# Merged slot loads, a five-step layer 0 and a new end in a four-layer graph-network kernel

## The chip, the core and the metric

The kernel runs on one core of a Trainium2 chip. The metric is the device time of one execution in microseconds (us); a comparison uses the median of several runs. The engines are TensorE (PE; weight loads are listed apart as PEld), VectorE (DVE), ScalarE (ACT), GpSimd (POOL) and SyncE (SP), which here only issues DMAs. The core has 16 DMA engines. A DMA that SP or ACT issues goes onto that engine's own queue, and instructions stand in the order of each engine's program.

## The reference

`reference(x, adj, ...)` takes 128 graphs of 64 nodes with 128 channels (x is 128 x 64 x 128) and a weighted adjacency (128 x 64 x 64) in which about a quarter of the entries are not zero and below 6. Four layers follow one another, each as `x = layernorm(x + layer(x))`:

- layer 0: a filter network over distances. Each entry d of adj becomes 20 Gaussians, exp(coeff d^2); these go through a 20 x 128 matrix, softplus, and a 128 x 128 matrix, and are multiplied by a cosine cutoff. The resulting filter W (one 128-vector per edge) multiplies the neighbour's features y = x w_in2f and is summed over neighbours; two dense layers follow.
- layer 1: the same with 64 Gaussians of other centres, other weights, and the entry of adj squared in place of the cutoff.
- layer 2: a two-hop graph convolution with elu, D^-1/2 (A + I) D^-1/2.
- layer 3: one normalised graph convolution with relu.

Everything is float32.

## The kernel before

Two graphs make a pair, which fills the 128 partitions: graph b on partitions 64b to 64b + 63. There are 64 pairs, in 8 sets of 8. Graphs are sorted by their number of edges, and within a graph the edges are compacted into "slots", so that only entries that count are worked on. A slot row holds, for all edges of one graph, the distance (d), the neighbour's index (j) and the weight (w). The slots per graph are `GSLOTS`: in layer 0 1080, 1092, 1044, 1020, 1008, 1008, 996 and 948 for the eight sets, in layer 1 1260, 1260, 1212, 1212, 1200, 1176, 1152 and 1140. Compaction writes the rows to DRAM; `later_loads` (L1365) reads them back per pair, each row broadcast over the partitions of its graph. In layer 0 a row of d is read in three thirds, each onto 20 (the last 24) partitions of the graph's 64, since 20 Gaussians are computed on each; in layer 1 onto all 64.

Before the steps, about 69 us load inputs and weights and compact the first set. Then `sparse_stack` (L613) runs a list of steps, the pairs two by two ("double pairs", 32 in each layer). A step takes a chunk of slots of both graphs. `chunks_of` (L68) gives the chunks: two per pair where the size is at most 1024 (layer 0, sets 3 to 7: four steps per double pair), three where it is more (sets 0 to 2: six steps), and in layer 1 five per double pair, whose middle step takes its slots from both pairs. A step is:

- `filter_in` (L1827): PE multiplies the Gaussians with the first matrix into PSUM (px), ACT takes Exp; `softplus` (ACT Ln);
- `gather` (L1856) of the step before: PE multiplies the features with a one-hot matrix (pg), ACT copies it (m<-pg); the one-hot matrix of a pair is made by DVE (`one_hot`, L1803) from j and w;
- `filter_out` (L1842) of the step before that: PE, second matrix (pw); `message` (L1882): DVE multiplies filter and features; `slot_sums` (L1912, L1916): DVE sums over the edges of each node.

`gaussians` (L1790) runs on ACT one to three pairs ahead. Beside the steps run generators that are advanced a few yields at a time: `early` (the compaction of later sets), `side`, `befores`, `nodes` and `convs` (dense layers per group of four pairs, layer norms, and layers 2 and 3 in `graph_convs`), `sums`, `last` (the same for the small groups at the end) and `stores`. `TURNS` says for each kind of step how far each is advanced, which pair's loads are issued (`load` for d, `late` for j and w, two or three pairs ahead) and which pair's Gaussians are computed. `in_order` (L648) makes each engine's order that of emission. The buffers: d and w three pairs deep, j two. In layer 1 the groups are of four pairs, except that the last set is split: q = 14 has pairs 0 to 3 of it, q = 15 two, 16 and 17 one each.

In the layer norm of a four-pair group (`layernorm`, L1448) GpSimd computes the reciprocal root with pow (L1460, L1461) and scales the four pairs (L1466); in the small groups ACT does it with Ln and Exp, and DVE scales. After the last step the remaining generators are advanced in turn until they are empty; all of them share two PSUM banks (`bank`, L1424). GpSimd writes the finished rows to their places in the output with indirect DMAs (L995).

Of the kernel before, what the change touches and what calls it, by code (L numbers as in the profile page):

```python
# [19 lines left out]
P = 128  # L20
# [46 lines left out]

def chunks_of(layer, size):  # L68

    if layer == 1:  # L70
        wide = -(-2 * size // 5)
        return (wide, wide, size - 2 * wide, size - 2 * wide, wide, wide)
    n = 2 if size <= 1024 else 3
    return (size // n,) * (2 * n)
# [538 lines left out]
def sparse_stack(ctx: ExitStack, tc: tile.TileContext, t: dict, out: bass.AP, flag):  # L613
# [122 lines left out]
    def dram_ap(ap, offset, dims):  # L736
        return bass.AP(tensor=ap.tensor, offset=ap.offset + offset, ap=dims)
# [118 lines left out]

    at_step = [0]

    def at_phase(k):
        while phase[0] not in (k, None):  # L860
            yield

    def steps_later(n):
        to = at_step[0] + n
        while at_step[0] < to:
            yield
# [498 lines left out]
    def later_loads(n):  # L1365


        layer, p = pair_at(n)
        s = p // 8
        size = GSLOTS[layer][s]  # L1370
        at = (p % 8) * 2 * size
        assert (layer, s) in stored, "slots are read before they are written"
        d = edge.tile([P, MAX_SLOTS], F32, tag="d", name=f"d_{n}", bufs=3)
        j = edge.tile([P, MAX_SLOTS], BF16, tag="j", name=f"j_{n}")
        w = edge.tile([P, MAX_SLOTS], F32, tag="w", name=f"w_{n}", bufs=3)

        def load(to, name, first, n):
            engine.dma_start(to, dram_ap(slots[layer, name][s], first, [[0, to.shape[0]], [1, n]]))  # L1378

        third = size // 3  # L1380
        d = d[:, 0 : size if layer else third]
        for b in range(2):
            rows, first = slice(A * b, A * (b + 1)), at + b * size
            engine = nc.sync
            if layer == 1:
                load(d[rows], "d", first, size)
            else:
                for k, end in enumerate((NG0, 2 * NG0, A)):
                    engine = nc.scalar if n == 0 and b * k == 0 else nc.sync
                    load(d[A * b + NG0 * k : A * b + end], "d", first + k * third, third)  # L1390

        def late():
            nonlocal engine
            engine = nc.sync
            for b in range(2):
                rows, first = slice(A * b, A * (b + 1)), at + b * size
                load(j[rows, 0:size], "j", first, size)
                load(w[rows, 0:size], "w", first, size)

        return (d, j, w), late  # L1400

# [19 lines left out]

    def bank(name, n=GS):  # L1424
        ps = ps_n.tile([P, 512], F32, tag="n", name=name)[:, 0 : n * P]
        return ps, ps.rearrange("p (s c) -> p s c", s=n)

# [7 lines left out]
    def tiled(name, n, q):  # L1435


        tag = f"c{q % 2}" if n == GS else f"c_{q}"
        return rings[0].tile([P, n * P], F32, tag=tag, name=f"{name}_{q}", bufs=4)

# [7 lines left out]
    def layernorm(y, dst, n, name, quick=False):  # L1448

        stats = node.tile([P, GS, 6], F32, tag="st", name=f"st_{name}", bufs=4)[:, 0:n]  # L1450
        mv = node.tile([P, GS, 2], F32, tag="mv", name=f"mv_{name}", bufs=4)[:, 0:n]
        for s in range(n):
            nc.vector.bn_stats(stats[:, s, :], y[:, s, :])
            nc.vector.bn_aggr(mv[:, s, :], stats[:, s, :])  # L1454
            if s + 1 == GS // 2 < n and not quick:
                yield
        rstd = node.tile([P, GS], F32, tag="rs", name=f"rs_{name}", bufs=4)[:, 0:n]
        yield
        if n == GS:
            nc.gpsimd.tensor_scalar(rstd, mv[:, :, 1], LN_EPS, None, ALU.add)  # L1460
            nc.gpsimd.tensor_tensor(rstd, rstd, neg_half[:, 0:n], ALU.pow)  # L1461
        else:
            act(rstd, mv[:, :, 1], AF.Ln, bias=ln_eps)
            act(rstd, rstd, AF.Exp, scale=-0.5)
        for s in range(n):
            (nc.gpsimd if n == GS else nc.vector).tensor_scalar(  # L1466
                dst[:, s, :], y[:, s, :], mv[:, s, 0:1], rstd[:, s : s + 1],
                ALU.subtract, ALU.mult,
            )
        yield  # L1470
# [128 lines left out]
    def node_after(layer, q, agg):  # L1599
# [48 lines left out]
        if layer == 1:  # L1648
            if n < GS:
                yield from graph_convs(q)  # L1650
            else:
                convs[q % 2].append(graph_convs(q))

    def elu(ps, bias, i, q, also=()):

# [40 lines left out]

        act(to, ps, AF.Copy)

    normals = {}

    def normals_of(q):

# [9 lines left out]
    def graph_convs(q):  # L1712
# [14 lines left out]
            return y  # L1727

        if n == GS:
            yield from at_phase(6)  # L1730
            scaled(2, q)
        flat, ps = bank(f"gx_{q}", n)
        for s in range(n):
# [17 lines left out]
        yield True  # L1751
        nT3 = by_pair(tiled("nTs3", n, q)) if n == GS else normals[3, q]
        h1 = yield from elu(flat, g["b1"], 1, q, normal(3, q, nT3) if n == GS else ())
        y2 = yield from times("hw2", lambda s: h1[:, s, :], lambda s: g["W2"])
        _, ps = bank(f"o2_{q}", n)
        for s in range(n):
# [4 lines left out]
        yield  # L1761
        yield from layernorm(z, xs, n, f"2_{q}")
        if n == GS:
            yield from at_phase(2)
        y3 = yield from times("sup", lambda s: xs[:, s, :], lambda s: nT3[:, s, :])
        flat, ps = bank(f"o3_{q}", n)
        nc.tensor.matmul(
# [153 lines left out]
            else:  # L1921
                nodes.append(node_after(layer, q, agg))

    befores, nodes, convs, sums = deque(), deque(), (deque(), deque()), deque()
    small_groups, small = range(NP // GS - 1, len(GROUPS[1])), {}
    at_end = range(NP // GS - 2, len(GROUPS[1]))
    last = {q: deque() for q in small_groups}
# [69 lines left out]
    def steps_of(n):  # L1997


        layer, p = pair_at(n)  # L2000
        size = GSLOTS[layer][p // 8]
        cuts, at = [], 0
        for m in CHUNKS[layer][p // 8]:
            cuts.append([part_of(n + at // size, at % size, at % size + m)])
            at += m
        if layer == 1:
            cuts[2:4] = [cuts[2] + cuts[3]]
        for k, cut in enumerate(cuts):
            yield dict(
                id=f"{n}_{k}", layer=layer, w=layers[layer], n=n, k=k, beat=len(cuts), parts=cut,  # L2010
                phase=k + p // 2 % 2 * len(cuts),
                size=sum(x["cols"][1] - x["cols"][0] for x in cut),
                starts=[x["n"] for x in cut if x["cols"][0] == 0],
            )
# [13 lines left out]
            gauss=((1, 0), (1, 1), None, (2, 0), (2, 1), None),  # L2028
            end=(7,) * 6,
        ),  # L2030
        4: dict(
            sums=(2, 3, 2, 2), early=(6, 7, 6, 7), side=(2, 3) * 2,
            late=(2, None, 3, None), load=(2, None, 3, None),
# [7 lines left out]
            end=(10,) * 5,  # L2041
        ),
    }
    FREE, MORE = 8, 0
    BEFORES = {6: (3, 4, 7, 8, 9), 4: (2, 3, 5, 6, 7), 5: (7, 8, 9)}

    block = nc.cur_bb.bb.instructions
    past = [None] * 2
# [1 line left out]
    for i in range(len(steps) + 2):  # L2050
        c, c1, c2 = steps[i] if i < len(steps) else None, *past
        now = c or dict(steps[-1], k=i - len(steps), phase=i - len(steps), starts=[])
        n, k, beat, layer = now["n"], now["k"], now["beat"], now["layer"]
        turn = {name: values[k] for name, values in TURNS[beat].items()}
        phase[0], at_step[0] = now["phase"] if n < N - FREE else None, i

        if n >= N - 4:
            run(sums, (2, 2, 5, 4, 2)[k] if c is not None else 9)
        else:
            run(sums, turn["sums"])  # L2060
        run(early, 9 if i < 18 else turn["early" if n < NP - 8 else "end"])
# [18 lines left out]
        if c is not None:  # L2080
# [4 lines left out]
            for part_ in c["parts"]:  # L2085
                m, (_, q) = part_["n"], part_["at"]
                if part_["cols"][0] > 0:
                    continue
                if m + GS < N:
                    ahead(m)  # L2090
                if part_["s"] == min(1, len(range(NP)[GROUPS[layer][q]]) - 1):
                    load_nodes(layer, q)
                if m > 0:
                    one_hot(m)
                if layer == 1 and part_["s"] == 0 and q in last:
                    last[q].append(normals_of(q))
            filter_in(c)
            if len(c["parts"]) == 2 and n + 3 < N:
                slot_data[n + 3], late_loads[n + 3] = later_loads(n + 3)
# [1 line left out]
            gather(c1)  # L2101
        if c is not None and turn["late"] is not None and n + turn["late"] < N:
            late_loads.pop(n + turn["late"])()
        if layer == 1 and befores and (n >= N - 8 or phase[0] in BEFORES[beat]):
            slot(befores)
        if c is not None:
            softplus(c)
            if beat % 2 == 0 and k % (beat // 2) == beat // 2 - 1 and sines:

                sines.popleft()()  # L2110
        if layer == 0:
            slot(nodes)
            if befores and phase[0] in BEFORES[beat]:
                slot(befores)
        if c2 is not None:
            filter_out(c2)
        for queue in last.values():
# [2 lines left out]
            slot(nodes)  # L2120
        if c2 is not None:
            message(c2)
        for _ in range(1 + (n >= N - MORE)):
            if convs[0]:
                slot(convs[0])
        if c is not None and turn["gauss"] is not None:
            m, stage = n + turn["gauss"][0], turn["gauss"][1]
            for stage in range(begun.get(m, 0), stage + 1 if m < N else 0):
                gaussians(m, stage)
                begun[m] = stage + 1  # L2130
        for _ in range(1 + (n >= N - MORE)):
            slot(convs[1])
        for queue in last.values():
            slot(queue)
        past = [c, c1]
    phase[0] = None
    run(sums, -1)
    while nodes or convs[0] or convs[1] or any(last.values()) or stores:
        for queue in (*last.values(), nodes, *convs):
            slot(queue)  # L2140
        run(stores, 1)
    in_order(first, block[-1], (nc.tensor, nc.scalar, nc.vector, nc.gpsimd, nc.sync))

# [46 lines left out]
```

## Time and profile before

| | |
|---|---|
| median of 3 runs | 1578.65 us (1576.26 to 1581.45) |
| the profiled execution | 1577.26 us |
| its span, first to last instruction | 1575.4 us |
| first step begins | 69.3 us |
| set 3 begins; layer 1 begins | 346.8; about 728 us |
| last message ends; last norm ends | 1512.1; 1568.75 us |

The page lists the busy time of each engine as a share of the span, then the busy share in slices, the DMA queues, the chain of work that ended last, and the costliest groups of instructions. A group's line gives the code line, engine and operation, output<-inputs, shapes, the number, then busy us and mean ns, then the engine's idle time just before them and what ended it. The view of stretches gives, for each stretch of the span, its length, each engine's busy time with the number of instructions, the granted TensorE clock, the busy share of the 16 DMA engines and the GB/s they moved. The trace further holds each DMA packet with its size and time, and each increment of a DMA's semaphore.

The double pairs of sets 0 to 2 begin 22.0 us apart (from 170.9 us on), those of sets 3 to 7 19.06 us, those of layer 1 23 to 24 us.

### The profile page before, as it was taken

The numbers are of one execution on the slowest core, as the hardware profiler recorded it, in microseconds if no ns is written. First come the engines' busy times: TensorE is split into PE (matmuls) and PEld (weight loads), VectorE is DVE, ScalarE is ACT, GpSimd is POOL, SyncE is SP. The second block draws the span as 40 slices with busy tenths as digits, with TensorE's granted clock in tenths as the row PEclk, the third lists the DMA queues.
The fourth block names the chain that finished last, engine by engine and source line by source line (L and its number), as shares of the span: only waits on it lengthen the run. The fifth ranks groups of instructions, "written<-read, shape, count | busy, mean of one in ns | idle before, by whom it ended". The sixth has DMA issues, their size and how long they took to land.

```text
span 1575.4 us, 23201 instructions
## 1 busy us (share of the span) xinstructions
PE 1427.4 (91%) x6841; PEld 790.8 (50%) x6841; DVE 1316.5 (84%) x2895; ACT 1313.8 (83%) x1647; POOL 759.3 (48%) x1175
## 2 busy tenths in 40 slices
PE   1387999999989999999999999999999999998974
PEld 1143454554444445554444555555555655554553
DVE  8796988888989899788788888888888888878763
ACT  1366897989888989899999999999999999988742
POOL 2435256365564545333912334555544665555544
PEclk9999999999999999999999999999999999999985
DMA  6766454545555545447665655555555555654100
GB/s 205 258 139 137 101 136 116 129 123 136 130 142 124 141 130 135 125 114 167 155 152 142 143 132 132 147 133 136 139 130 138 139 132 131 150 132 106 31 7 23
DMA packets 122280, 205.60 MB, mean 131 GB/s; under 512 B 47956, under 2 KB 80034, under 8 KB 121506
## 3 DMA queue, kind: packets, MB, share of 16 engines
q1 hardware_dynamic: 113330, 188.40, 48.2%
q0 software_dynamic: 6576, 14.99, 2.9%
q8 instruction: 57, 0.93, 0.3%
q10 hardware_dynamic: 2240, 0.65, 0.2%
q14 instruction: 77, 0.63, 0.1%
HBM read 185.29 MB, written 18.64 MB: 129 GB/s over the span
## 4 chain that ended last, share of the span: by engine, by line
PE 61%; ACT 11%; DVE 9%; DMA 6%; issue 4%; SPq 2%; POOL 2%; another core or an unknown queue 1%; DVEq 0%; ACTq 0%; POOLq 0%
PE pw L1842 23%; PE px L1827 13%; PE pg L1856 11%; ACT h L955 5%; DVE m L1882 2%; DMA w<-w_dram 2%; DVE agg L1912 2%; DMA j<-j_dram 2%; ACT d L955 2%; PE y L1491 1%; PE hw L1722 1%; SPq L1378 1%; PE u L1615 1%; PE back L1641 1%; PE o L1632 1%
## 5 line engine op out<-in xcount | busy, mean ns | idle before, releaser
L955 ACT ACTIVATE h<-h,half 128x1008 f32<-128x1008 f32 (+12 forms) x313 | 332.8, 1063 | 0.1
L955 ACT ACTIVATE m<-pg 128x1008 f32<-128x1008 f32 (+12 forms) x313 | 291.8, 933 | 46.1 <-DVE agg L1916 21.0
L1856 PE MATMUL pg<-w,ys 64*128 64x504 f32 (+15 forms) x1376 | 299.4, 518 | 27.0 <-ACT d L955 7.5
L1842 PE MATMUL pw<-h,w_L_gnn_W2T 128*128 128x504 f32 (+8 forms) x640 | 300.2, 592 | 2.6 <-DVE m L1882 2.4
L1882 DVE SCALAR_TENSOR_TENSOR m<-pw,c_L_gnn_b,m 128x1008 f32<-128x1008 f32 (+8 forms) x161 | 194.8, 1211 | 113.6 <-PE pw L1842 97.7
L1912 DVE TENSOR_REDUCE agg<-m 128x32 f32<-128x544 f32 (+14 forms) x455 | 287.2, 669 | 1.8 <-PE u L1615 0.4
L1842 PE MATMUL pw<-h,w_L_gnn_fw 128*128 128x504 f32 (+6 forms) x608 | 253.6, 540 | 9.7 <-DVE m L1882 7.7
L1882 DVE SCALAR_TENSOR_TENSOR m<-pw,c_L_gnn_fb,m 128x1008 f32<-128x1008 f32 (+6 forms) x152 | 168.8, 1111 | 69.9 <-PE pw L1842 47.2
L955 ACT ACTIVATE h<-px,c_L_gnn_b 128x1008 f32<-128x1008 f32 (+8 forms) x160 | 171.4, 1071 | 30.2 <-PE px L1827 30.0
L955 ACT ACTIVATE h<-px,c_L_gnn_fb 128x1008 f32<-128x1008 f32 (+6 forms) x152 | 148.2, 975 | 53.8 <-PE px L1827 37.9
L1856 PEld LDWEIGHTS pg<-w,ys 64*128 64x128 f32 x1376 | 129.0, 189 | 118.6 <-issue 50.3
L1842 PEld LDWEIGHTS pw<-h,w_L_gnn_W2T 128*128 128x128 f32 x640 | 109.4, 191 | 153.5 <-issue 82.0
L1803 DVE SCALAR_TENSOR_TENSOR w<-j,row,w 128x1212 f32<-128x1212 bf16 (+12 forms) x128 | 181.3, 1416 | 5.4 <-DMA w<-w_dram 5.4
L1827 PE MATMUL px<-d,fw 64*128 64x168 f32 (+10 forms) x928 | 155.4, 440 | 27.1 <-DMA d<-d_dram 18.4
L1827 PE MATMUL px<-d,w1t 64*128 64x504 f32 (+11 forms) x768 | 173.1, 542 | 0.5 <-ACT h L955 0.4
L1460 POOL TENSOR_SCALAR rs<-mv 128x4 f32<-128x4 f32 x61 | 15.0, 245 | 288.7 <-DVE mv L1454 288.0
L1842 PEld LDWEIGHTS pw<-h,w_L_gnn_fw 128*128 128x128 f32 x608 | 105.3, 193 | 90.9 <-issue 44.9
L1827 PEld LDWEIGHTS px<-d,fw 64*128 64x128 f32 x928 | 74.4, 189 | 127.8 <-issue 36.1
L955 ACT ACTIVATE d<-d,neg_off 128x1212 f32<-128x1212 f32 (+12 forms) x128 | 120.9, 945 | 8.2 <-DMA d<-d_dram 8.2
L995 POOL DMA_INDIRECT rows<-comb,goes x64 | 71.0, 1110 | 108.9 <-DMA rows<-comb,goes 64.5
L1466 POOL TENSOR_SCALAR x_all<-ny,mv,rs 128x128 f32<-128x128 f32 x124 | 109.2, 889 | 3.3
L995 POOL DMA_INDIRECT out_dram<-gz,at_row x56 | 75.1, 1341 | 60.1 <-DMA out_dram<-gz,at_row 55.0
(264 smaller groups left out, 2300.8 us busy)
## 6 DMA issues: line engine op xcount, KB each, us to landing
d<-d_dram SPq DMA_DIRECT2D x32, 315.0 KB
w<-w_dram SPq DMA_DIRECT2D x32, 315.0 KB
d<-d_dram SPq DMA_DIRECT2D x32, 303.0 KB
w<-w_dram SPq DMA_DIRECT2D x32, 303.0 KB
w<-w_dram SPq DMA_DIRECT2D x32, 252.0 KB
j<-j_dram SPq DMA_DIRECT2D x32, 157.5 KB
j<-j_dram SPq DMA_DIRECT2D x32, 151.5 KB
d<-d_dram SPq DMA_DIRECT2D x16, 300.0 KB
```

The lines of the kernel that those rows point to most:

```text
L955: latest = nc.scalar.activation(out_, in_, func, **kw)
L995: nc.gpsimd.indirect_dma_start(out=into, out_offset=bass.IndirectOffsetOnAxis(ap=at, axis=0), in_=rows, in_offset=None,)
L1378: engine.dma_start(to, dram_ap(slots[layer, name][s], first, [[0, to.shape[0]], [1, n]]))
L1466: (nc.gpsimd if n == GS else nc.vector).tensor_scalar(dst[:, s, :], y[:, s, :], mv[:, s, 0:1], rstd[:, s : s + 1], ALU.subtract, ALU.mult,)
L1491: nc.tensor.matmul(ps[:, s, :], lhsT=xt[:, s * P : (s + 1) * P], rhs=w["win"], start=True, stop=True)
L1615: nc.tensor.matmul(by[:, s, :], lhsT=w["o1"], rhs=of, start=layer == 1, stop=True)
L1803: nc.vector.scalar_tensor_tensor(hots[n][:, 0:size], j[:, 0:size], near, wt[:, 0:size], ALU.is_equal, ALU.mult)
L1827: nc.tensor.matmul(ps[:, b, at : at + m], lhsT=w["w1"][rows, :] if c["layer"] else w["w1"][rows, k, :], rhs=d[rows, col : col + m], start= ...
L1842: nc.tensor.matmul(c["pw"][:, b, :], lhsT=c["w"]["w2"], rhs=c["h"][:, b, :], start=True, stop=True)
L1856: nc.tensor.matmul(ps[:, b, to], lhsT=y[rows, :], rhs=hots[part_["n"]][rows, first:stop], start=True, stop=True,)
L1882: nc.vector.scalar_tensor_tensor(to, c["pw"][:, :, of], c["w"]["b2"], to, ALU.add, ALU.mult)
L1912: nc.vector.tensor_reduce(av[:, :, :, r], both, AX.X, ALU.add)
```

## The change

Three things are changed together.

**A. Loads.** A load of j or w, and in layer 1 of d, brings the rows of both graphs at once: the source pattern gets an outer dimension of two graphs, the target is all 128 partitions. In layer 0 the first two thirds of a graph's d come in one load onto 40 partitions, the last third in one onto 24. A pair then has 6 loads in layer 0 instead of 10, and 3 instead of 6 in layer 1. Of pair 0's d loads, ACT's queue issues one instead of four.

**B. Sets 0 to 2 of layer 0** are cut like layer 1, into five steps per double pair with a middle step from both pairs (of 432 + 432 + (216 + 216) + 432 + 432 slots for size 1080), with turns of their own (`TURNS[3]`, `BEFORES[3]`).

**C. The end.** Norms of four-pair groups that fall to the end go to ACT and DVE as those of the small groups do; the convolutions of q = 14 get a queue and tiles of their own; normals of the small groups are begun earlier; phases are kept until four pairs before the end; after the steps six halves of the steps' PSUM banks serve the six queues, and a written list of turns says in which order these are advanced.

```diff
 def chunks_of(layer, size):
-    if layer == 1:
+    if layer == 1 or size > 1024:
         wide = -(-2 * size // 5)
...
-        def load(to, name, first, n):
-            engine.dma_start(to, dram_ap(slots[layer, name][s], first, [[0, to.shape[0]], [1, n]]))
+        both = [[size, 2], [0, A], [1, size]]
+
+        def load(to, name, first, dims):
+            engine.dma_start(to, dram_ap(slots[layer, name][s], first, dims))
...
-        for b in range(2):
-            rows, first = slice(A * b, A * (b + 1)), at + b * size
-            engine = nc.sync
-            if layer == 1:
-                load(d[rows], "d", first, size)
-            else:
-                for k, end in enumerate((NG0, 2 * NG0, A)):
-                    engine = nc.scalar if n == 0 and b * k == 0 else nc.sync
-                    load(d[A * b + NG0 * k : A * b + end], "d", first + k * third, third)
+        engine = nc.sync
+        if layer == 1:
+            load(d, "d", at, both)
+        else:
+            for b in range(2):
+                first = at + b * size
+                load(d[A * b : A * b + 2 * NG0], "d", first, [[third, 2], [0, NG0], [1, third]])
+                engine = nc.scalar if n == 0 and b == 0 else nc.sync
+                load(
+                    d[A * b + 2 * NG0 : A * (b + 1)], "d", first + 2 * third,
+                    [[0, A - 2 * NG0], [1, third]],
+                )
+                engine = nc.sync
 
         def late():
-            nonlocal engine
-            engine = nc.sync
-            for b in range(2):
-                rows, first = slice(A * b, A * (b + 1)), at + b * size
-                load(j[rows, 0:size], "j", first, size)
-                load(w[rows, 0:size], "w", first, size)
+            load(j[:, 0:size], "j", at, both)
+            load(w[:, 0:size], "w", at, both)
...
+    own_banks, now_run = {}, [None]
+    own_names = [f"{i}_{NP // GS - 2}" for i in (1, 2, 3)]
+
     def bank(name, n=GS):
+        if own_banks:
+            ps = own_banks[now_run[0]][:, 0 : n * P]
+            return ps, ps.rearrange("p (s c) -> p s c", s=n)
...
-        if n == GS:
+        apart = n == GS and not own_banks and name not in own_names
+        if apart:
             nc.gpsimd.tensor_scalar(rstd, mv[:, :, 1], LN_EPS, None, ALU.add)
...
-            (nc.gpsimd if n == GS else nc.vector).tensor_scalar(
+            (nc.gpsimd if apart else nc.vector).tensor_scalar(
...
+        3: dict(
+            sums=(2, 2, 1, 2, 2), early=(5, 6, 5, 6, 6), side=(2, 2, 3, 2, 3),
+            late=(2, None, None, 3, None), load=(2, None, 3, None, None),
+            gauss=((1, 1), None, (2, 0), (2, 1), (3, 0)),
+            end=(7,) * 5,
+        ),
...
-    FREE, MORE = 8, 0
-    BEFORES = {6: (3, 4, 7, 8, 9), 4: (2, 3, 5, 6, 7), 5: (7, 8, 9)}
+    FREE, MORE, ONCE, FAST = 4, 4, 1, (0, 0)
+    SUMS = (2, 2, 3, 4, 4)
+    EARLY = {N - gap: q for gap, q in zip((14, 11, 8), small_groups)}
+    BEFORES = {6: (3, 4, 7, 8, 9), 4: (2, 3, 5, 6, 7), 5: (7, 8, 9), 3: (3, 4, 6, 7, 8)}
...
     run(sums, -1)
-    while nodes or convs[0] or convs[1] or any(last.values()) or stores:
-        for queue in (*last.values(), nodes, *convs):
-            slot(queue)
+    run(nodes, -1)
+    for pool, tag, keys in ((ps_x, "x", "zy"), (ps_g, "g", "ab"), (ps_w, "w", "xc")):
+        both = pool.tile([P, 2, 512], F32, tag=tag, name=f"own_{tag}")
+        for h, key in enumerate(keys):
+            own_banks[key] = both[:, h, :]
+    queues = dict(zip("xyz", last.values()), n=nodes, a=convs[0], b=convs[1], c=convs[2])
...
+    while any(queues.values()):
+        for key in turns:
+            now_run[0], size = key, len(block)
+            while queues[key] and len(block) == size:
+                run(queues[key], 1)
+            run(stores, 1)
+        turns = "zyxcba"
+    while stores:
         run(stores, 1)
```

## The prediction

> **What bounds the kernel now.** I read the busy table first, then the chain of waits, then the busy time by stretches, then the DMA records, because the change rewrites every load of the step loop.
>
> ```profile
> PE 1427.4 (91%) x6841; PEld 790.8 (50%) x6841; DVE 1316.5 (84%) x2895; ACT 1313.8 (83%) x1647; POOL 759.3 (48%) x1175
> PE 61%; ACT 11%; DVE 9%; DMA 6%; issue 4%; SPq 2%; POOL 2%; another core or an unknown queue 1%; DVEq 0%; ACTq 0%; POOLq 0%
> ```
>
> TensorE is busy and leads the chain; DMA holds 6% of it. The stretches (columns: length; PE, PEld, DVE, ACT, POOL busy; clock; DMA share of 16 engines; GB/s) say where:
>
> ```profile
> 69.00:347.00 278.00, 248.72 (x1167) 133.71 (x1165) 234.71 (x663) 223.22 (x322) 128.81 (x191) 0.97 0.54 128
> 347.00:728.00 381.00, 363.91 (x1816) 190.91 (x1817) 341.52 (x831) 337.19 (x417) 185.02 (x321) 1.00 0.52 132
> 900.00:1400.00 500.00, 498.01 (x2481) 290.39 (x2481) 424.08 (x723) 468.79 (x548) 263.72 (x294) 1.00 0.54 136
> 1512.00:1576.00 64.00, 35.19 (x163) 27.32 (x161) 29.61 (x105) 19.99 (x60) 29.77 (x38) 0.69 0.06 18
> ```
>
> In layer 1 (900 to 1400) TensorE has 2 us idle in 500. In layer 0's sets 0 to 2 (69 to 347) all engines have gaps. The last 64 us are a chain of small pieces. The column to look at for this change is DMA: loads keep **16 DMA engines** busy 52 to 54% of the time. If the same bytes went through fewer engines, that share would pass 1 below nine of them.
>
> **Part A, the merged loads: how many engines carry one?** The new source pattern is [[size, 2], [0, 64], [1, size]] against 128 partitions; before it was [[0, 64], [1, size]] against 64. The trace records each increment of a DMA's semaphore, so I counted. The 64-row loads of w and j give 16 increments, spread over the landing. The 20-row loads of d give 11: one 0.5 to 0.7 us after issue, ten between 1.6 and 2.1 us. So 16 and 10 engines, and the missing ones are credited at once. Before has five loads of exactly the new form, a source of three dims onto plain partitions. L1954 loads caps (128 partitions) from [[18, 8], [0, 16], [1, 18]]: 9 increments, one at 1.11 us, eight from 2.15 to 2.54. The four loads of L792 (60 partitions, source [[0, 3], [1, 20], [1, 1]]) give 4 each, one and three. The 128 partitions of caps did not make it 16: the **outer source dim** did, 8 and 3. The new loads have 2 there. So I take two engines for each merged load of j, w and d; the 24-row loads of d stay as they are.
>
> In the Trainium skill, "DMA: Bandwidth & Descriptors", section "Why a DMA increments its semaphore by 16 and not by 1", the number of engines is the largest k up to 16 that divides the slowest dim of both patterns, and they are the lowest-numbered k; that speaks against this change. It makes 2 of these loads, as the five rows do, and always the same two, which the sum below takes from another row.
>
> Are they the same two each time? Between 64.75 and 65.74 us the six d loads of pair 0 are in flight on two queues, each on 8 to 10 engines:
>
> ```profile
> 64.75:65.74 0.99, 0.00 (x0) 0.00 (x0) 0.46 (x1) 0.85 (x1) 0.99 (x1) 1.00 0.52 146
> 12.00:18.00 6.00, 0.00 (x0) 0.00 (x0) 5.73 (x10) 0.00 (x0) 0.00 (x0) 1.00 1.01 424
> 1022.00:1024.00 2.00, 2.00 (x14) 1.43 (x14) 1.52 (x2) 1.86 (x2) 0.00 (x0) 1.00 1.03 242
> ```
>
> The share is 0.52, about 8 of 16, with work queued for six times ten: had each load taken other engines, it would near 1. So they queue on the same ones.
>
> What does one engine carry? At 12 to 18 us all 16 are full with 424 GB/s, 26.5 each. In the loop's bursts they are full at 242, 15 each; but the first packets of a burst (one row is one packet) take 185 ns for 4800 B and 156 for 4032, and the later ones of 16 competing engines 355. Two engines don't compete with 14 others, so I take 185/4800 = **0.0386 ns per byte**; 355/4800 is a rival.
>
> Per pair of size S, each of the two engines moves 64 rows of 4S (w), 64 of 2S (j), twice 20 of 4S/3 (d), and its share of the 24-row loads, 6 rows of 4S/3: 445 S bytes in layer 0. In layer 1 d, w and j make 64 x 10 S = 640 S.
> - Layer 0, S = 1080: 481 KB, 18.6 us per pair; compute takes 22.0/2 = 11.0 us there and 19.06/2 = 9.5 in sets 3 to 7 (starts of steps). Layer 1, S = 1200: 768 KB, 29.7 us against 11.6.
> - The eight sizes of layer 0 add up to 8196 slots, of layer 1 to 9612, each for 8 pairs: 445 x 65,568 x 0.0386 = **1127 us**, 640 x 76,896 x 0.0386 = **1900 us**.
>
> This cannot hide. j has two buffers and w three, so at most some two pairs' loads wait in the queue; prefetch moves them, but a pair needs 19 or 30 us of two engines whatever the lead.
>
> What is added: before the first load 64 us (first d load at 63.3). Other DMA: the shares give (0.54 x 278 + 0.52 x 381) = 348 us per engine in layer 0, of which packets of slot loads took 241 and others the rest; by the packets one by one the others are 111 us there and 30 in layer 1, 141 in all, which the two engines carry too (at uncontended packet times an estimated 60). After the last w has landed: three steps of 4.7 us and the pipeline, about 19, then the tail, 48 (below), and 6.6 to the span's end plus 1.9 to the run's time: 75. Stalls: every SP load now queues behind the slot loads for 20 to 40 us instead of landing in 2 to 5, and SP is in order, so an ad, zr or x load that DVE or PE needs stops them; what sits behind on SP (the next j and w, which wait for one_hot) then goes out late. The gap of one is an issue and a first landing, 0.55 + 2.4 us, 3 us; there are some 30 such groups of loads: 90 us, with 0 and 128 pairs x 3 = 384 as ends. DVE and ACT wait in order behind them, without a price of their own, since all wait for the loads anyway.
>
> Sum: 64 + 1127 + 1900 + 141 + 75 + 90 = **3397 us**, against 1577.3 of the profiled execution (span 1575.4) and 1578.65, the median, 1.4 above it. I say 3400.
>
> **Part B, five steps for six** (sets 0 to 2, 12 double pairs, 72 steps to 60). From rows by width: px, pg, pw of a 360-column step 0.69 + 0.69 + 1.27 = 2.65 us, of a 432-column one, between that and 504 columns (3.65), 3.15; 5 x 3.15 against 6 x 2.65, so PE gains 0.15. ACT gains 15.1 - 14.4 = 0.7 us, DVE 0.3, and each step loses about 0.44 us to hand-over (22.0 us against 15.9 + 3.4 of node work). 12 x 0.7 makes -8; early gets 28 turns for 24, about 1 us more DVE per double pair (+12 at worst). Alone: -8, ends -20 and +5. Under loads of 18.6 us a pair it is hidden: 0 here.
>
> **Part C, the end.** From the last message to the last norm 56.65 us pass (1512.10 to 1568.75). On the chain:
>
> ```profile
> 1524.60 1.05 POOL rs L1461
> 1525.74 3.13 POOL x_all L1466 x4
> 1529.05 2.37 DMA out_dram<-gz,at_row
> ...
> 1543.19 2.38 DMA out_dram<-gz,at_row
> ```
>
> A GpSimd norm of four pairs is 0.24 + 1.05 + 3.13 = 4.4 us; on ACT and VectorE, at the small groups' rows, 0.3 + 0.2 + 4 x 0.3 = 1.7. But DVE then has 43 us of work after the last message (rows of the new order at these durations) where it had 30, and GpSimd eight stores of 2.6. I take 48 for 56.65: -9, and -3 for steps freed before. Ends 0 and -18. Here the tail comes after the last load, so -9 stays in the 75.
>
> **Rivals.**
> 1. All 16 engines share a merged load (faster). Then load packets take what they did, 241 + 380 = 621 us per engine of 1575, SP issues 448 fewer at 0.33 to 0.56 us off the chain (A: -4; at most -21 by PE's idle in sets 3 to 7), and B and C count: 1577 - 4 - 8 - 12 = 1553. Against: the five counted loads. It decides from six engines on: layer 1's 1.54 MB x 0.0386 / k is under 11.6 us from k = 6, layer 0's 0.96 MB under 11.0 from k = 4. 5%.
> 2. Two engines, but other ones from load to load (faster). w takes 64 x 0.167 = 10.7 us, j 5.6, side by side, within two pairs' lead of 20 us; only the first pair shows it, +10: 1563. Against: the 0.52. 4%.
> 3. Two engines at the contended 355 ns: 3027 x 355/185 = 5809; 64 + 5809 + 141 + 75 + 90 = 6179. Against: those packets belong to full bursts. 5%.
>
> **The numbers.** The forecast has 86%. Its range: from 26.9 GB/s (430 of the best microsecond, 2917), 60 of other DMA and no stall, 64 + 2917 + 60 + 75 = 3116, to 174 ns per 4032 B (their median, 3385), 141 and 384 of stalls: 4049. That leaves out 5% of its own cases and the rivals. A measurement tells 0.3% (4.7 us) from no change. Slower 0.91, same 0.01, faster 0.08.
>
> **What would show it.** Increments of a merged load: 3 (one, then two). DMA share near 2/16 = 0.12 to 0.2, not 0.54; about 50 GB/s in the loop. PE under 50% busy; first waits DVE w <- DMA w at one_hot and ACT d <- DMA d. Pairs 18 to 20 us apart in layer 0, 29 to 32 in layer 1. Steps 5 per double pair without gain; tail 45 to 50 us. I am wrong if w's landing shows 16 increments within 5 us, or if w packets of 4800 B take well over 200 ns.

## The result and the profile after

The changed kernel takes 3391.91 us (median of 4; 3390.92 to 3396.83) against 1578.79 us: 2.149 times as long, interval 2.1449 to 2.1531. The profiled execution took 3396.83 us, its span is 3395.0.

The page after, busy times, chain of waits and the first DMA queue. Read the chain first: DMA held 6% of it before, now 83%. TensorE stands for almost half of the span, the other engines for more; and queue q1 moved the same 188 MB in packets that take 15.3% of 16 engines' span, where they took 48.2% of a span less than half as long.

```profile
PE 1790.0 (53%) x6984; PEld 962.6 (28%) x6985; DVE 1321.5 (39%) x2907; ACT 1320.2 (39%) x1623; POOL 667.4 (20%) x1139
...
q1 hardware_dynamic: 101516, 188.44, 15.3%
...
DMA 83%; SPq 6%; DVE 3%; PE 3%; ACT 3%; issue 1%; POOL 0%; ACTq 0%; DVEq 0%; POOLq 0%
```

Who waited for whom, after (us in total, times, longest). The two longest waits for DMA are the first readers of d and w; I take the waits of DVE m for PE, and their like, to follow from them.

```profile
ACT d L957 <- DMA d<-d_dram: 1757.3, 120, 23.3
...
DVE w L1823 <- DMA w<-w_dram: 887.5, 122, 21.2
DVE m L1902 <- PE pw L1862: 742.6, 140, 19.0
```

The stretches, after: layer 0's loads, layer 1's loads, and the end from the last message to the last norm (columns as in the prediction; the last three are clock, DMA share, GB/s).

```profile
72.00:1407.00 1335.00, 753.61 (x3113) 407.21 (x3109) 575.04 (x1492) 554.45 (x700) 299.57 (x524) 0.76 0.19 63
1407.00:3311.00 1904.00, 968.11 (x3552) 503.49 (x3552) 630.30 (x1023) 716.58 (x811) 325.08 (x401) 0.72 0.14 55
3340.00:3389.00 49.00, 32.03 (x174) 27.92 (x174) 38.44 (x140) 22.61 (x72) 10.73 (x13) 0.78 0.05 15
```

A share of 0.14 is 2.2 of 16 engines, at 55 GB/s in all. The trace's other records say the same of single loads. A merged load increments its semaphore 3 times: j of pair 0, issued at 65.5 us, at 0.94, 9.67 and 9.72 us after issue. The last two of w of pair 0 (issued at 66.1 us) come 19.68 and 19.72 us after. A row of 4800 B takes 185 ns (median and the middle half of 2048 packets; 296 before). From 1500 to 3200 us exactly two packets of slot loads are in flight in 94% of the time, three in 4%, none in 0.3%: **the same two engines, full, at 25.9 GB/s each**.

### The profile page after: what moved, and what is told of

Same layout as the page of the kernel before. It is cut to its first block, busy times and chain, and to the rows that moved or that the text cites. A ratio compares the mean times of both kernels' runs of the same rounds, so it can differ in the third digit from the quotient of the medians.

```text
span 3395.0 us, 22554 instructions
## 1 busy us (share of the span) xinstructions
PE 1790.0 (53%) x6984; PEld 962.6 (28%) x6985; DVE 1321.5 (39%) x2907; ACT 1320.2 (39%) x1623; POOL 667.4 (20%) x1139
## 3 DMA queue, kind: packets, MB, share of 16 engines
q1 hardware_dynamic: 101516, 188.44, 15.3%
## 4 chain that ended last, share of the span: by engine, by line
DMA 83%; SPq 6%; DVE 3%; PE 3%; ACT 3%; issue 1%; POOL 0%; ACTq 0%; DVEq 0%; POOLq 0%
DMA d<-d_dram 55%; DMA w<-w_dram 25%; SPq L1382 4%; DMA x_all<-x_sorted 1%; ACT d L957 1%; SPq L1181 1%; ACT h L957 1%; SPq L1413 1%; PE pw L1862 1%; PE pg L1876 1%; DMA j_dram<-jc 1%; PE px L1847 0%; DVE w L1823 0%; DMA a_all<-adj_sorted 0%; DVE m L1902 0%
## 5 line engine op out<-in xcount | busy, mean ns | idle before, releaser
L1876 PE MATMUL pg<-w,ys 64*128 64x504 f32 (+15 forms) x1376 | 410.5, 681 | 501.7 <-DVE w L1823 499.0
L1847 PE MATMUL px<-d,w1t 64*128 64x504 f32 (+11 forms) x768 | 230.0, 697 | 430.4 <-ACT h L957 430.4
L1862 PE MATMUL pw<-h,w_L_gnn_W2T 128*128 128x504 f32 (+8 forms) x640 | 358.2, 689 | 5.2 <-DVE m L1902 4.9
L1876 PEld LDWEIGHTS pg<-w,ys 64*128 64x128 f32 x1376 | 159.5, 243 | 628.1 <-issue 373.0
L1862 PE MATMUL pw<-h,w_L_gnn_fw 128*128 128x504 f32 (+8 forms) x560 | 289.5, 645 | 15.1 <-issue 12.0
L957 ACT ACTIVATE m<-pg 128x1008 f32<-128x1008 f32 (+11 forms) x301 | 287.0, 954 | 14.0 <-PE pg L1876 13.2
L1847 PE MATMUL px<-d,fw 64*128 64x168 f32 (+22 forms) x1120 | 168.1, 422 | 193.4 <-ACT h L957 172.0
L1902 DVE SCALAR_TENSOR_TENSOR m<-pw,c_L_gnn_fb,m 128x1008 f32<-128x1008 f32 (+8 forms) x140 | 166.4, 1188 | 219.2 <-PE pw L1862 206.0
L1847 PEld LDWEIGHTS px<-d,w1t 64*128 64x128 f32 x768 | 74.1, 228 | 484.3 <-ACT h L957 450.8
L957 ACT ACTIVATE h<-px,c_L_gnn_fb 128x1008 f32<-128x1008 f32 (+8 forms) x140 | 144.5, 1032 | 68.4 <-PE px L1847 53.0
```

The lines of the kernel that those rows point to most:

```text
L957: latest = nc.scalar.activation(out_, in_, func, **kw)
L1847: nc.tensor.matmul(ps[:, b, at : at + m], lhsT=w["w1"][rows, :] if c["layer"] else w["w1"][rows, k, :], rhs=d[rows, col : col + m], start= ...
L1862: nc.tensor.matmul(c["pw"][:, b, :], lhsT=c["w"]["w2"], rhs=c["h"][:, b, :], start=True, stop=True)
L1876: nc.tensor.matmul(ps[:, b, to], lhsT=y[rows, :], rhs=hots[part_["n"]][rows, first:stop], start=True, stop=True,)
L1902: nc.vector.scalar_tensor_tensor(to, c["pw"][:, :, of], c["w"]["b2"], to, ALU.add, ALU.mult)
```

## The experiments

Theory 1 is the prediction's: the outer source dimension sets the number of DMA engines. Theory 2 is the rival: the new order of steps and turns, or the size of the loads. Ratios are to the kernel before in the same series of runs, on the same chip; its own median was 1567.6 and 1566.6 us in two of the series and 1579.5 in the third (see the end), so where a per cent counts, ratios are compared and not times.

### Parts B and C without A

```diff
-        both = [[size, 2], [0, A], [1, size]]
...
+            engine.dma_start(to, dram_ap(slots[layer, name][s], first, [[0, to.shape[0]], [1, n]]))
```

> The changed kernel with the loads of before (64 rows each): parts B and C alone. Theory 1 (the loss is the number of DMA engines that a merged load runs on): the loss is gone and B and C are worth what they are worth without it, 1577 - 8 - 12 = about 1557, between 1545 and 1575; the slot loads show 16 increments. Theory 2 (the loss comes from the new order of the steps and turns: loads asked for later, engines waiting in order): it stays well above 1579, and in sets 0 to 2 above all.

Measured: 1555.45 us, ratio 0.9923 [0.9906, 0.9939]. The whole loss is part A; theory 2's first half falls.

### Part A alone

The same edit the other way round: the new `later_loads` in the kernel before.

> Before with the merged loads alone. Theory 1: the same DMA bound as in the changed kernel with the old tail, about 3392 + 9 = 3400, within 3350 to 3450; two engines full in layer 1. Theory 2: most of the loss is missing, well below 3000.

Measured: 3405.89 us, ratio 2.1729 [2.1686, 2.1773], 14 us above the changed kernel. Part A makes the loss without B and C.

### The pattern without the merging: 4, 8 and 2 engines

These three are the kernel before, with 64-row loads as they are; only the way the same bytes are written down differs (k = 4, 8, 2).

```diff
-            engine.dma_start(to, dram_ap(slots[layer, name][s], first, [[0, to.shape[0]], [1, n]]))
+            rows = to.shape[0]
+            dims = [[0, k], [0, rows // k]] if rows == A else [[0, rows]]
+            engine.dma_start(to, dram_ap(slots[layer, name][s], first, [*dims, [1, n]]))
```

> Before with its 64-row loads as they are, the same bytes and number of loads, and only the source pattern written as [[0, 4], [0, 16], [1, n]] in place of [[0, 64], [1, n]]. Theory 1: 5 increments per load, four engines: layer 1 carries 320 S bytes per engine and pair, 320 x 76,896 x 0.0386 = 950 us plus 30 of others instead of 780; layer 0 with (192 + 19) S = 533 us plus 111 of others just under its 660, with stalls 660 to 750. 64 + 700 + 980 + 84 = about 1830, between 1780 and 1950. Theory 2 (size or order, not the pattern): 1579.

Measured: 2064.52 us, ratio 1.3171 [1.3126, 1.3217], with 5 increments per load. Layer 1 takes 993 us for the expected 980; layer 0 takes 931 where 660 to 750 was expected.

> The same with [[0, 8], [0, 8], [1, n]]. Theory 1: 9 increments, eight engines, 290 + 111 us of work in layer 0's 660 and 475 + 30 in layer 1's 780: hidden, 1579 within 10 us. Theory 2: 1579 too; it is there to show from what number on the engines decide (six by the prediction).

Measured: 1687.13 us, ratio 1.0766 [1.0748, 1.0784], 9 increments. The number of engines is as expected, but the loss is not gone: layer 0 takes 713 us, layer 1 839 for 780. Layers 0 and 1 with four engines, then with eight:

```profile
70.00:1001.00 931.00, 713.65 (x2989) 378.24 (x2991) 581.43 (x1503) 564.79 (x743) 295.71 (x513) 0.87 0.34 91
1001.00:1994.00 993.00, 827.93 (x3649) 452.23 (x3646) 654.34 (x1086) 721.94 (x831) 384.30 (x436) 0.92 0.26 104
```

```profile
69.00:782.00 713.00, 628.25 (x2994) 330.72 (x2993) 579.66 (x1498) 562.26 (x743) 304.37 (x512) 0.97 0.46 120
782.00:1621.00 839.00, 784.37 (x3646) 439.50 (x3645) 655.09 (x1091) 719.71 (x832) 391.72 (x437) 0.96 0.43 122
```

With four engines in layer 1 the share is 0.26, 4 of 16 and hardly any idle: a bandwidth bound, as expected, and 104 GB/s is 4 x 26. Three things were missing in my sum. First, in layer 0 SyncE's queue waits for the DMA eight before it. Its own waits with four engines, 450 to 1000 us:

```profile
SPq L1380 <- DMA w<-w_dram: 151.9, 59, 4.0
SPq L1380 <- DMA j<-j_dram: 34.9, 34, 2.0
```

In the kernel before the first of these is 16.8 us in all. A DMA of SyncE takes one of eight semaphores in turn (numbers 101 to 108 in the trace), so eight are in flight at most; with ten loads per pair that is less than a pair, and the engines run dry: with four engines, in 15% of layer 0 no packet of a slot load is in flight.

Second, with eight engines the packets themselves are slower: a 4800 B row takes 279 ns (median), where four engines take 185. So 160 S bytes of a layer 1 pair take 192,000 x 279/4800 = 11.2 us, almost the 11.6 that a pair had. But the pairs are now 13.1 us apart (839/64), and the DMA share is 0.43 where eight full engines make 0.50, so this alone does not set the pace. Third, GpSimd's indirect stores of finished rows (out_dram) land later. Before, then with eight engines:

```profile
POOL out_dram L995 <- DMA out_dram<-gz,at_row: 55.0, 28, 3.0
```

```profile
POOL out_dram L995 <- DMA out_dram<-gz,at_row: 106.9, 34, 7.7
ACT gy_hw L955 <- DMA out_dram<-gz,at_row: 50.3, 9, 9.9
```

In layer 1 these stores hold 23.3% of the chain with eight engines and no load holds as much as 1.4%; ACT has no such wait before, and its 50 us are about what the layer is longer (839 for 784). No run takes the stores away to prove it.

> Before with its 64-row loads of j, w and layer 1's d, nothing merged, and their source pattern written as [[0, 2], [0, 32], [1, n]]; d of layer 0 stays on its 8 to 10 engines. Theory 1 (engines and bytes alone): two engines carry (384 + 19) S in layer 0 = 1019 us and 640 S = 1900 in layer 1; 64 + 1019 + 1900 + 141 + 84 + 90 = 3298. Theory 1 with what the run of four engines showed (its layer 0 took 931 us where engines needed 644: SP waits for the DMA eight before, and ten loads per pair fill the eight lanes): layer 0 about 1019 + 111 + 290 = 1420, 3430 in all; then merging as such is a gain of some 60 us under two engines. Theory 2 (merging to 128 rows is what costs): near 1579.

Measured: 3490.28 us (one run). Theory 2 falls: without any merging two engines cost as much and more. The term for the eight semaphores fits too: layer 0 takes 1434 us (1420 expected), 85 more than in part A alone, although its two engines have fewer bytes there. There SyncE's slot loads wait 395 us for w and j loads before them with ten loads per pair, 228 with six. With the number of engines held at two, merging as such is a gain, as far as one run tells.

### Part A with 16 engines

Behind a set's stores its rows are copied eight times in DRAM, so that the outer dimension of a merged load can be 16 (with part C; set 0 and d of layer 0 as before).

```diff
+            for name in "djw"[1 - layer :]:
+                nc.sync.dma_start(
+                    dram_ap(copies[layer, name][s], 0, [[8 * n, 16], [n, 8], [1, n]]),
+                    dram_ap(slots[layer, name][s], 0, [[n, 16], [0, 8], [1, n]]),
+                )
...
+            from_ = dram_ap(copies[layer, name][s], 8 * at, [[size, 16], [0, 8], [1, size]])
```

> Part C, and part A with its outer dimension made 16: behind the stores of a set (all but the first) one DMA per array copies each graph's row of j, w and layer 1's d eight times in DRAM (40 more DMAs in the kernel), and a load of both graphs reads [[size, 16], [0, 8], [1, size]] onto 128 partitions. d of layer 0 and set 0 load as before. Theory 1: 16 increments, and the loss is gone although the loads bring both graphs; 9 DMAs fewer in ten pairs' dozens on SP are off the chain, so between C alone (0.989 of before) and 10 us less; landings of the merged w within 6 us. Rival (a 128-row load costs by itself, by its size): well above C alone, over 1600 us. The copies themselves move some 40 MB more and hold SP for some us per set: up to +10.

Measured: 1572.36 us, ratio 1.0037 [1.0024, 1.0050], against 0.9893 for C alone. The loads bring both graphs, with 16 increments, and in layer 1 w lands 4.5 to 7.8 us after its issue (5.4 as the median); the factor of two is gone, so size is not the cause. But the run is 1.4% (23 us) above C alone, where at most 10 were expected, and merging gains nothing that can be seen. Layer 1 with merged loads, then with separate ones (C alone):

```profile
743.00:1516.00 773.00, 759.71 (x3634) 425.22 (x3632) 651.40 (x1081) 716.87 (x831) 382.08 (x425) 1.00 0.51 131
```

```profile
731.00:1503.00 772.00, 758.77 (x3634) 424.22 (x3632) 650.60 (x1081) 717.41 (x832) 385.83 (x425) 1.00 0.53 131
1503.00:1551.00 48.00, 31.64 (x175) 27.16 (x174) 38.02 (x141) 22.75 (x72) 10.79 (x13) 0.81 0.05 15
```

TensorE's share is the same; half the loads buy 0 us where TensorE has no gap. The 23 us lie in layer 0: 15 in sets 3 to 7 (399 us for 384), most of the rest in the last double pair before them (29.5 us for 23.7). The copies add traffic there; I take them to be the cost, but no run has the copies without the merged loads.

### B alone, C alone, and one piece of A

B alone takes `chunks_of`, the cuts, `TURNS[3]` and `BEFORES[3]`; C alone is the changed kernel with old loads and these two lines as they were:

```diff
-    if layer == 1 or size > 1024:
+    if layer == 1:
...
-        if len(cuts) == 6 and (True):
+        if layer == 1:
```

> Before with part B alone (sets 0 to 2 in five steps, old loads, old end). The prediction's -8 us, ends -20 and +5, with set 3 beginning some 8 us earlier and nothing changed behind it. Rival: early's four more turns and the shorter lead of the loads eat it: within 3 us of before.

Measured: 1585.56 us, ratio 1.0045 [1.0027, 1.0063]: 0.45% slower. From 176 to 351 us the eight double pairs take 21.86 us each where they took 21.99; the first takes 30.2 instead of 25.8, and sets 3 to 7, whose steps B does not change, 390.5 instead of 384.7.

> Before with part C alone (the end anew, old loads, six steps in sets 0 to 2). The prediction's -12 us, ends 0 and -18: last message to last norm 48 to 50 us instead of 56.65, and some 3 us before the last message. Rival: DVE's 43 us after the last message hold the end at 54 or more: -3.

Measured: 1562.35 us, ratio 0.9893 [0.9873, 0.9913], **the lowest of all**, though its interval still touches that of parts B and C together. Last message to last norm: 48.2 us for 56.65. The last message ends 9 us earlier (1503.1 for 1512.1).

> Parts B and C with one piece of part A: the first two thirds of d in layer 0 in one 40-row load on two engines. Two engines then carry (53 + 48 + 8) S bytes, 4.6 us of a pair's 9.5 to 11: theory 1 says hidden, within 4 us of B and C alone (ratio 0.9923), SP's 128 issues of 0.33 us being off the chain. Rival (a merged load costs by itself, since it lands later whatever its engines): slower than B and C alone by over 10 us.

```diff
+                engine.dma_start(
+                    d[A * b : A * b + 2 * NG0],
+                    dram_ap(slots[layer, "d"][s], first, [[third, 2], [0, NG0], [1, third]]),
+                )
```

Measured: 1575.40 us, ratio 0.9972 [0.9957, 0.9987], 0.5% above B and C alone: between the two expectations. 3.2 us are seen at once: the first step begins at 73.1 instead of 69.9. In the changed kernel, whose d loads are the same, the 40-row load of pair 0 issued at 64.2 lands 4.7 us later, where the 20-row ones took 1.8 to 2.1. With the stall of 9.8 us near 150 us taken off (see the end), layer 1 begins 10 us later than in parts B and C; 2.5 more of them come in the first double pair (31.9 us for 29.4), the rest in small pieces. From there to the end the two take the same (within 3 us). So the loss lies in layer 0, where the merged loads are; what makes it is not settled.

## Why the prediction was right, and where it was not

The mechanism and the time were right (3400, measured 3392); the terms came out so:

| term | predicted, us | measured in the profiled execution, us |
|---|---|---|
| up to the first load of j and w | 64 | 66 to 68 |
| layer 0: loads, other DMA, stalls | 1127 + 111 + 90 = 1328 | 1340 (j and w from 67.9 to 1407.5) |
| layer 1: loads, other DMA | 1900 + 30 = 1930 | 1904 (1407.2 to 3311) |
| after the last w | 75 | 86 |
| sum | 3397 | 3396.8 |

That the two sums agree to 0.2 us is chance: the rows are off by +3, +12, -26 and +11, which cancel.

- **Number of engines.** Five small loads of the kernel before with a source of the same form carried the whole forecast; k = 2, 4, 8 and 16 gave 3, 5, 9 and 16 increments. The rule of the Trainium skill ("DMA: Bandwidth & Descriptors", section "Why a DMA increments its semaphore by 16 and not by 1") agrees with all four. One reading was wrong, at little cost: the 24-row loads of d give 13 increments, so 12 engines and not 8, and each engine has 4 of their rows per pair and not 6 (2.7 S of the 445 S bytes).
- **Rate.** The first packets of a burst were the right row: 185 ns, not the 355 of rival 3.
- **The same two engines**: two packets in flight, 94% of the time; rival 2 falls.
- **Layer 0** held as a sum, and its parts are not all measured. Other packets took 92 us (mean of 16 engines) for 111. The loads were more than 1127, since small rows cost more per byte: by median packet times they come to an estimated 1161 us (a 2016 B row of j 82 ns, 0.0407 ns per byte), by mean times to 1248. That leaves 0 to 87 us for stalls, where I had 90. The price I gave a stall (a missing first landing) is not shown; what the queue shows is SyncE's wait for the DMA eight before, which the prediction does not name: 183 us before slot loads here. Pairs came 20.9 us apart in layer 0, where I had said 18 to 20.
- **Layer 1** is its loads alone, 1904 us for 1900; the 30 of other DMA did not come on top.
- **After the last w**: 28.6 us to the last message where I had 19; the tail itself was 49.0 for 48.
- **"It decides from six engines on" was wrong.** At eight the kernel is 7.7% slower. The step took the uncontended packet time, and no account of SyncE's order or of the stores that share the engines.
- **Part B, -8: wrong**, it is +0.45%, about +7. The step that failed is "each step loses about 0.44 us to hand-over", so that fewer steps would gain. TensorE's idle time in a double pair was 1.2 us before and is 1.5 with one step fewer (windows 170.9 to 346.8 and 176 to 351), so it does not go by the step. TensorE did lose 0.4 us of work per double pair, although px now takes 40 matmuls for 24, because the new cuts fall inside the thirds in which d is stored; but the double pairs hardly changed (21.99 to 21.86). The longer first double pair cost 4.4 us, sets 3 to 7 another 5.8; why they do is open.
- **Part C, -12: measured -1.07%, about -17.** The tail was right (-8.4 for -9), the 3 us for freed steps were 9, 1 of them a shorter stall (see the end).
- **Part A by rival 1, -4: 0** in layer 1, as the run with 16 engines shows (773 us for 772); in layer 0 a gain can't be told from the cost of the copies.
- "PE under 50% busy": 53%. Its time rose from 1427 to 1790 us for nearly the same work, see below.

## What to carry to other kernels

Before two loads become one, write down the outer dimension of both patterns as the instruction will carry them: it sets how many DMA engines share the load, and a broadcast over two graphs makes it 2. The number of increments in any trace that has one DMA of that form tells it without a run: here one more than the engines, or 16 for 16. Halving the number of loads gained nothing where TensorE had no gap. Of the versions here the new end alone has the lowest ratio, and part B alone is slower than before.

## What the runs showed of the hardware that was not expected

- **An issue takes long when the DMA engines are far behind.** SyncE's timeline in layer 1, after (start, duration): an issue takes 6 to 12 us, where it took 0.45 to 0.6.

```profile
2010.03 11.73 SPq L1382 DMA_DIRECT2D w<-w_dram  x1
2021.86 6.32 SPq L1382 DMA_DIRECT2D d<-d_dram  x1
2028.28 11.59 SPq L1382 DMA_DIRECT2D j<-j_dram  x1
```

When the issue of w ends at 2021.8, its last increment is 21.8 us away, and until then each of the two engines starts 148 rows: 64 of j and 84 of d and w. So I read the long issue as waiting for room among some 150 rows; that there is such a limit is my reading, and no run tests it.

- **A starved TensorE runs at a lower clock.** In layer 1 TensorE is busy for 51% of the time after and its granted clock is 0.72; it is 0.92 at 83% (four engines), 0.96 at 93% (eight) and 1.00 at 98% (C alone). Its busy time in the whole kernel is a quarter more.
- **Packet time rises with the number of engines at work.** A 4800 B row takes 185 ns with two or four engines, 279 with eight, 296 with 16, and 301 with 16 on all 128 partitions and eight copies of each row (medians). So that many engines read one row, or write the same 64 partitions, is not the reason; what they compete for stays open.
- **The kernel before differs by 12 us between series of runs**, on one chip 1567.6 and 1579.5. In its profile DVE stands for 9.9 us from about 145 us on, TensorE and ACT for most of that, while GpSimd goes on; the waits put it down to something outside the core or to a queue that they don't know:

```profile
DVE m L1882 <- remote: 9.9, 1, 9.9
```

The profiles of C alone (8.9), B alone (9.2) and of parts B and C with the merged d loads (9.8) have it; those of B and C with old loads and of the 16-engine loads, taken where before needed 1567 us, have no such row. Each ratio above is to before in the same series. The cause stays open.
